# Regrouping the register loads of a column copy on VectorE and ScalarE in a graph layer

## The chip, the cores and the metric

The kernel runs on one core of one Trainium2 chip. The metric is the device time of one execution in microseconds (us). Five engines work side by side, each through its own list of instructions in order: TensorE (PE, with its weight loads PEld), VectorE (DVE), ScalarE (ACT), GpSimd (POOL) and SyncE (SP), which only issues DMAs. Besides instructions for its engine, such a list holds some that the engine's sequencer runs itself, register loads for instance; the profile gives them with a q behind the engine's name (DVEq) and does not count them as busy.

## The reference

One layer of a graph network over 12500 nodes with 64 numbers each and 212500 directed edges with 32 numbers each. The edges are sorted by destination (`dst`). All is float32.

```python
msg_in = jnp.concatenate([nodes[row], nodes[col], edge_features], axis=-1)   # row = src, col = dst
messages = relu(msg_in @ mW1 + mb1) @ mW2 + mb2
aggregated = jax.ops.segment_sum(messages, col, num_segments=nodes.shape[0])
upd = relu(jnp.concatenate([nodes, aggregated], -1) @ uW1 + ub1) @ uW2 + ub2
out = layernorm(x + upd)
```

## The kernel before

The edges are cut into 554 groups (`G`) of 384, three tiles of 128 (`TG`). A loop over `k` makes one step a group. A chain runs through each group, and one step holds work on three groups: `turn(k)`, `hidden(k - 2)` and `sums(k - 4)`.

- Gather (line 167, GpSimd). One indirect DMA a tile fetches the source nodes' 64 numbers of 128 edges into a ring of 20 groups (`own_s`, `RING`). `gather(k + 16)` is issued in step `k` and waits until TensorE has transposed the group that last held the ring's place, 20 groups earlier.
- `turn` (line 378, TensorE) transposes a group's three tiles, source nodes and one-hot places together, so that the edges stand in columns; ScalarE brings the result from PSUM to SBUF (line 389, `own_st`). A group's first tile can be left out of the gathers ("columned", below); then only its places are moved, and ScalarE needs two instructions.
- `hidden` (line 404, TensorE) multiplies by `mW1`, the window of 32 destination nodes' projections (`own_wm`) and the edges' numbers; VectorE applies the ReLU (line 415).
- `sums` (line 431, TensorE) sums the group's edges into its window of 32 nodes; VectorE adds the window to `own_agg` at an address from a register (line 458). Every fourth step also counts the edges a node has (line 442), and VectorE adds four windows of counts (line 463), each waiting for the one before.
- VectorE also makes the one-hot places of a later group (line 366).

All that TensorE does in a step waits at its first matmul: for the gathers of group `k`, for the DMAs, and for what VectorE and ScalarE did with its results two steps earlier.

The source nodes of a columned group's first 128 edges aren't gathered. All nodes lie in SBUF as columns (`own_xc`), and VectorE and ScalarE copy one column after another to its place in `own_st`, 64 partitions of 4 bytes (lines 565 and 567). The address of a column stands in a register, and the registers are filled from a list in SBUF (`index`) by `registers` (line 546): one load instruction for as many registers as it names. `fetch` then makes the copies. `VCOLS` and `ACOLS` say how many columns VectorE and ScalarE copy in a step, load by load; `COLS` is their sum. Columns are copied from step `BEGIN` = 18 until ten steps before the end, and `COPIED` (line 86) lists the groups for which a place in time is found: one group for each 128 columns. Every eighth step a new piece of the list comes by DMA (line 525, SP's queue), and VectorE turns it into addresses (line 531).

VectorE's list in a step before: ReLU (415), load of 12 (546), addition (458), in every fourth step four count additions (463), 12 copies (565), places (366), load of 8, 8 copies. The load of 12 stands between the ReLU and the addition, through the list `between`: a function put there ahead of the step is called within `add` (line 456). ScalarE's list: eviction (389), load of 12, 12 copies, load of 12, 12 copies.

As the groups close, 25 parts of the output are computed between the steps (lines 474 to 516). In the first 25 steps ScalarE also evicts a projection of all nodes (line 343), from which the windows are read. The last ten steps have no columns to copy and go through the three parts one after another.

Of the kernel before, what the change touches and what calls it, by code (L numbers as in the profile page):

```python
# [48 lines left out]
TIMES = 4  # L49
BEGIN = 18  # L50
CHECKED = 8
VCOLS = (12, 8)
ACOLS = (12, 12)
COLS = sum(VCOLS + ACOLS)
SPAN = 8


def tiles_of(g):

    n = min(GE, E - g * GE)  # L60
    return [min(P, n - j * P) for j in range((n + P - 1) // P)]
# [53 lines left out]
def ordered(ctx: ExitStack, tc: tile.TileContext, a, own, ok):  # L115
# [26 lines left out]
    def after(first, *others):  # L142

        tc.declare_no_dep(first.ins, group="quiet", reason="waits for the last of a step")
        for i in others:
            tc.add_manual_dep(
                first.ins, i.ins.name,
                mybir.DependencyInfo(mybir.DependencyClass.Sync, mybir.DependencyReason.DATA),
                reason="the kernel's own rings",
            )  # L150
        return first
# [69 lines left out]
    def bit(k):  # L221

        nodes = [NEAR_NODES + (N - NEAR_NODES) * i // BITS for i in (k, k + 1)]
        tiles = [first + (NT - first) * i // BITS for i in (k, k + 1)]
        nc.sync.dma_start(src_sb[:, slice(*tiles)], a["src"][:, slice(*tiles)])
        nc.sync.dma_start(xc[:D, slice(*nodes)], a["xT"][:, slice(*nodes)])
# [51 lines left out]
    def combined():  # L278

        wps = ups.tile([H, CH], F32, name="u_ps").rearrange("p (n h) -> p n h", n=4)  # L280
        nc.tensor.matmul(wps[:, 0], w2t, u1s, start=True, stop=True)
        nc.tensor.matmul(wps[0:1, 1], b2, u1s, start=True, stop=True)
        nc.vector.tensor_copy(wc, wps[:, 0])
        nc.vector.tensor_copy(ux[COUNT : COUNT + 1, :], wps[0:1, 1])
# [27 lines left out]
    def inputs(b):  # L312
        if b * SB >= G:
            return
        c0, c1 = b * SB * GE, min(E, (b + 1) * SB * GE)
        efs_by[b] = nc.sync.dma_start(own.st[b % BLOCKS][D + W :, : c1 - c0], a["efT"][:, c0:c1])
        after(efs_by[b], *([hidden_by[(b - BLOCKS + 1) * SB - 1]] if b >= BLOCKS else []))
# [17 lines left out]
    def projected(c):  # L335

        base, n = TABLE[c]
        ps = ups.tile([H, CH], F32, name="u_ps").rearrange("p (n h) -> p n h", n=4)
        for j in range(n):
            nc.tensor.matmul(ps[:, j], xc[: D + 1, base + j * P :][:, :P], w1b,  # L340
                             start=True, stop=True)
        t = rowp.tile([P, 4, H], F32, name="t")
        nc.scalar.activation(t[:, :n], ps[:, :n], AF.Copy)  # L343
        written.append(after(nc.sync.dma_start(
            by_dst[base : base + n * P, :].rearrange("(n p) h -> p n h", n=n), t[:, :n])))
# [79 lines left out]
    def sums(g, ps):  # L425
        h, s = own.h[g % NH], own.s[g % RING]
        sizes = tiles_of(g)
        sg = ps[2][:, : TIMES * W].rearrange("p (t w) -> p t w", w=W)
        did = []
        for j, p in enumerate(sizes):  # L430
            did.append(nc.tensor.matmul(  # L431
                sg, h[:p, j, :],
                s[:p, j, D:].unsqueeze(1).to_broadcast([p, TIMES, W]),
                start=j == 0, stop=j == len(sizes) - 1))
        counts = []
        if g % SB == SB - 1 or g == G - 1:
            g0 = g // SB * SB
            whole = [q for q in range(g0, g + 1) if tiles_of(q) == [P] * TG]
            at_ps = ps[2][0:1, TIMES * W :][:, : SB * W].rearrange("o (q w) -> o q w", w=W)
            first_s = g0 % RING  # L440
            for j in range(TG):
                did.append(nc.tensor.matmul(  # L442
                    at_ps[:, : len(whole)], own.one,
                    own.ring[:, first_s : first_s + len(whole), j, D:],
                    start=j == 0, stop=j == TG - 1))
            if len(whole) < g + 1 - g0:
                for j, p in enumerate(sizes):
                    did.append(nc.tensor.matmul(
                        at_ps[:, len(whole)], own.one[:p], s[:p, j, D:],
                        start=j == 0, stop=j == len(sizes) - 1))  # L450
            counts = [(q, at_ps[:, q - g0]) for q in range(g0, g + 1)]

        def add(step):
            sums_by[g] = step
            at = bass.ds(starts[g], W)
            if between:
                between.pop()()
            did = [after(nc.vector.tensor_tensor(agg[:, at], sg[:, 0, :], agg[:, at], ALU.add),  # L458
                         step)]
            for q, counted in counts:  # L460
                counted_by[q] = step
                count = xc[COUNT : COUNT + 1, bass.ds(starts.pop(q), W)]
                did.append(after(nc.vector.tensor_tensor(count, counted, count, ALU.add), step))  # L463
            return did

        return did, [*relu_by[g], *copy_by[g]], add
# [53 lines left out]
    def indexes(i):  # L520

        n = min(SPAN * COLS, P * len(COPIED) - i * SPAN * COLS)
        if n > 0:
            indices[i] = ixp.tile([1, SPAN * COLS], I32, name="index")
            nc.sync.dma_start(indices[i][:, :n], a["src_copied"][:, i * SPAN * COLS :][:, :n])

    def addresses(i):

        if i in indices:
            t = indices[i][:, : min(SPAN * COLS, P * len(COPIED) - i * SPAN * COLS)]  # L530
            nc.vector.tensor_scalar(t, t, 4.0, float(own.at), ALU.mult, ALU.add)

    def registers(k, *parts):

        i, n = divmod(k - BEGIN, SPAN)
        if i < 0:
            return
        all_parts = [*((ET.DVE, c) for c in VCOLS), *((ET.Activation, c) for c in ACOLS)]
        for part in parts:
            engine, count = all_parts[part]  # L540
            c0 = (k - BEGIN) * COLS + sum(c for _, c in all_parts[:part])
            count = min(count, P * len(COPIED) - c0)
            if count <= 0:
                return
            b = c0 - i * SPAN * COLS
            _, v = nc.values_load_multi_w_load_instructions(  # L546
                indices[i][0:1, b : b + count], engines=[engine],
                min_val=own.at, max_val=own.at + 4 * (N - 1),
                skip_runtime_bounds_check_because="a source is one of the nodes",
            )  # L550
            held[part] = engine, c0, v
# [60 lines left out]
        window(g)  # L612
    indexes(0)
    made = summed = 0
    between, held = [], {}

    for k in range(G):
        if k < BITS:
            bit(k)
        if 1 < k < len(TABLE):  # L620
            projected(k)
        if k == CHECKED:
            addresses(0)
            combined()
            ordered_edges()
            early.close()
            up = ctx.enter_context(tc.tile_pool(name="upd", bufs=2))
        if k % SB == 2:
            inputs(k // SB + 2)
        if k % SB == 1:  # L630
            places(k // SB + 1)
        if k < G - SHORT:
            between.append(lambda: registers(k, 0))
            step((turn, k), *([(hidden, k - 2)] if k > 1 else []),
                 *([(sums, k - 4)] if k > 3 else []))
            made, summed = max(0, k - 1), max(0, k - 3)
            if between:
                between.pop()()
            fetch(0)
        else:  # L640

            step((turn, k))
            for _ in range(2):
                if summed < made:
                    step((sums, summed))
                    summed += 1
            for _ in range(2):
                if made <= k:
                    step((hidden, made))
                    made += 1  # L650
        window(k + SB)
        onehot(k + LEAD)
        if k < G - SHORT:
            for part in range(1, len(VCOLS + ACOLS)):
                registers(k, part)
                fetch(part)
            if k >= BEGIN and (k - BEGIN) % SPAN == 0:
                indexes((k - BEGIN) // SPAN + 1)
            if k >= BEGIN and (k - BEGIN) % SPAN == SPAN - 2:
                addresses((k - BEGIN) // SPAN + 1)  # L660
        if k + AHEAD < G:
            gather(k + AHEAD)
# [330 lines left out]
```

## Time and profile before

| | |
|---|---|
| median of 3 runs | 1879.1 us (1875.58 to 1879.48) |
| profiled execution | 1872.44 us, span 1870.6 us |
| VectorE busy | 1452.9 us (78%), 13141 instructions |
| ScalarE busy | 1558.7 us (83%), 13374 instructions |
| TensorE busy | 1302.0 us (70%), weight loads 1139.3 us (61%) |
| GpSimd busy | 1400.1 us (75%), of it 1481 gathers 1399.4 us |
| column copies | 10480 on VectorE, 12560 on ScalarE |

The span is the time from the first to the last instruction; the profiled execution's own time contains it. Busy times overlap. In a row of a group stand the line, engine, operation and tiles, the count, the busy time, the mean length of one in ns, and after the second bar the engine's idle time just before these instructions with what ended it; "issue" means that the profile shows nothing that was waited for. Instructions of one engine overlap by their ends: VectorE's copies last 190 ns each, but their busy time is 884.5 us for 10480.

### The profile page before, as it was taken

To read this page: it belongs to the slowest core of one execution; us is meant where nothing else is said; L and a number is where in the kernel's file an instruction comes from. 1 tells how busy PE (TensorE), PEld (TensorE's weight loads), DVE (VectorE), ACT (ScalarE), POOL (GpSimd) and SP (SyncE) were. 2 spreads that over 40 slices of the span, in tenths; PEclk is the share of its full clock that TensorE was granted. 3 is DMA by queue.
4 is the path that set the end of the run, shared out by engine and by line. 5 is a ranking of instruction groups with operands and counts; after the bars stand their busy time and mean duration, and the time that the engine had idled before them with its cause. 6 is when DMAs were issued, how large, how long until landed. Compare 5 with 4: busy or idle time off the path is not lost. (4 is left out here: it accounts for less than half of the span.)

```text
span 1870.6 us, 55967 instructions
## 1 busy us (share of the span) xinstructions
PE 1302.0 (70%) x9839; PEld 1139.3 (61%) x9839; DVE 1452.9 (78%) x13141; ACT 1558.7 (83%) x13374; POOL 1400.1 (75%) x1488
## 2 busy tenths in 40 slices
PE   1777777677767667677676776776767767667676
PEld 0676666666666556566665666665656656556665
DVE  1338888899897888877887878888878888888773
ACT  5249999999998888888888888888888888888871
POOL 7777777777777777777777777777777777777774
PEclk9889999999999998998999998999998999999999
DMA  4543222222222222222222222222222222222221
GB/s 93 138 123 75 54 54 54 51 54 53 52 54 48 50 52 49 50 49 45 54 52 47 52 46 54 48 51 48 53 46 53 45 54 51 48 53 48 50 49 26
DMA packets 112796, 104.10 MB, mean 56 GB/s; under 512 B 51586, under 2 KB 82960, under 8 KB 112432
## 3 DMA queue, kind: packets, MB, share of 16 engines
q0 software_dynamic: 47392, 48.60, 14.8%
q1 hardware_dynamic: 64196, 51.35, 10.0%
q14 instruction: 280, 2.29, 0.4%
q8 instruction: 84, 1.38, 0.3%
q10 hardware_dynamic: 844, 0.48, 0.1%
HBM read 90.61 MB, written 9.62 MB: 54 GB/s over the span
## 5 line engine op out<-in xcount | busy, mean ns | idle before, releaser
L167 POOL DMA_INDIRECT own_s<-in_x,src_sb x1481 | 1399.4, 945 | 452.5 <-issue 342.9
L567 ACT ACTIVATE own_st<-own_xc 64x4 uint8 x12560 | 1265.6, 192 | 60.2 <-issue 52.2
L565 DVE COPY own_st<-own_xc 64x4 uint8 x10480 | 884.5, 190 | 17.3 <-issue 9.2
L378 PE MATMUL own_ps<-own_ident,own_s 128*96 128x128 f32 x1661 | 294.1, 288 | 488.7 <-DMA own_s<-in_x,src_sb 164.0
L378 PEld LDWEIGHTS own_ps<-own_ident,own_s 128*96 128x96 f32 x1661 | 169.1, 131 | 593.5 <-issue 291.0
L431 PE MATMUL own_ps<-own_s,own_h 128*128 128x128 f32 x3322 | 490.3, 287 | 1.2 <-DVE own_h L415 0.6
L404 PE MATMUL own_ps<-own_wm,own_st 128*128 128x128 f32 x3322 | 485.5, 285 | 0.0
L415 DVE TENSOR_SCALAR own_h<-own_ps 128x384 f32<-128x384 f32 x553 | 302.1, 547 | 185.5 <-PE own_ps L442 84.7
L431 PEld LDWEIGHTS own_ps<-own_s,own_h 128*128 128x128 f32 x3322 | 443.3, 203 | 2.3 <-DVE own_h L415 1.2
L404 PEld LDWEIGHTS own_ps<-own_wm,own_st 128*128 128x128 f32 x3322 | 437.8, 201 | 1.8 <-issue 1.2
L389 ACT ACTIVATE own_st<-own_ps 96x384 f32<-96x384 f32 (+2 forms) x734 | 294.2, 401 | 167.5 <-PE own_ps L442 81.6
L458 DVE TENSOR_TENSOR own_agg<-own_ps,own_agg 128x32 f32 x554 | 105.8, 191 | 170.6 <-DVE own_h L415 90.4
L366 DVE TENSOR_TENSOR own_s<-iota,dlc 128x96 f32<-128x96 f32 x554 | 136.2, 247 | 0.3 <-issue 0.2
L442 PE MATMUL own_ps<-own_s,own_one 128*1 128x128 f32 x834 | 120.6, 283 | 0.0
L463 DVE TENSOR_TENSOR own_xc<-own_ps,own_xc 1x32 f32 x554 | 101.9, 184 | 18.5 <-DVE own_xc L463 1.8
L442 PEld LDWEIGHTS own_ps<-own_s,own_one 128*1 128x1 f32 x834 | 60.2, 85 | 35.7 <-issue 3.6
L340 PE MATMUL u_ps<-w1b,own_xc 65*128 65x128 f32 x196 | 33.4, 323 | 58.1 <-ACT t L343 38.8
L340 PEld LDWEIGHTS u_ps<-w1b,own_xc 65*128 65x128 f32 x196 | 29.1, 227 | 62.3 <-ACT t L343 42.1
L343 ACT ACTIVATE t<-u_ps 128x512 f32<-128x512 f32 (+1 forms) x25 | 14.7, 588 | 58.2 <-DMA by_dst<-t 37.9
L487 PE MATMUL u_ps<-same,own_xc 65*128 65x64 f32 (+1 forms) x196 | 37.0, 271 | 1.5 <-ACT u L480 1.4
L489 PE MATMUL u_ps<-u,u 128*128 128x64 f32 (+1 forms) x196 | 38.0, 276 | 0.0
L487 PEld LDWEIGHTS u_ps<-same,own_xc 65*128 65x128 f32 (+1 forms) x196 | 29.7, 191 | 2.3 <-ACT u L480 2.2
(62 smaller groups left out, 257.1 us busy)
## 6 DMA issues: line engine op xcount, KB each, us to landing
own_st<-in_efT SPq DMA_DIRECT2D x138, 192.0 KB
own_s<-in_x,src_sb POOLq DMA_INDIRECT x1481
own_wm<-by_dst SPq DMA_DIRECT2D x554, 16.0 KB
by_dst<-t SPq DMA_DIRECT2D x24, 256.0 KB
out<-o SPq DMA_DIRECT2D x24, 128.0 KB
own_xc<-in_xT SPq DMA_DIRECT2D x12, 179.2 KB
index<-in_src_copied SPq DMA_DIRECT2D x65, 1.4 KB
dlc_i<-in_dst_cols SPq DMA_DIRECT2D x1, 831.0 KB
```

Of the source, the lines that this page charges most:

```text
L167: nc.gpsimd.indirect_dma_start(out=s[:p, j, :D], out_offset=None, in_=x[:, :], in_offset=bass.IndirectOffsetOnAxis(ap=src_sb[:p, g * TG + ...
L366: places_by[g] = nc.vector.tensor_tensor(own.s[g % RING][:, :, D:], iota.unsqueeze(1).to_broadcast([P, TG, W]), dlc[:, g * TG : (g + 1) * ...
L378: nc.tensor.transpose(xt[:, j * P : j * P + p], s[:p, j, :], ident[:p, :p])
L389: after(nc.scalar.activation(t[r, c : c + n][:, m], xt[r, m], AF.Copy), step))
L404: nc.tensor.matmul(pre[:p, j, :], t[:, c + j * P : c + j * P + p], wm[g % NW], start=True, stop=True)
L415: relu_by[g] = [nc.vector.tensor_scalar(h, pre, 0.0, None, ALU.max)]
L431: did.append(nc.tensor.matmul(sg, h[:p, j, :], s[:p, j, D:].unsqueeze(1).to_broadcast([p, TIMES, W]), start=j == 0, stop=j == len(sizes) - 1))
L442: did.append(nc.tensor.matmul(at_ps[:, : len(whole)], own.one, own.ring[:, first_s : first_s + len(whole), j, D:], start=j == 0, stop=j == ...
L458: did = [after(nc.vector.tensor_tensor(agg[:, at], sg[:, 0, :], agg[:, at], ALU.add), step)]
L463: did.append(after(nc.vector.tensor_tensor(count, counted, count, ALU.add), step))
L565: by[engine] = nc.vector.tensor_copy(o, x_at)
L567: by[engine] = nc.scalar.activation(o, x_at, AF.Copy)
```

## The change

VectorE copies 24 columns a step where it copied 20, in three loads of eight registers for one of twelve and one of eight. ScalarE copies 28 where it copied 24, in loads of 12, 8 and 8 for two of 12. `COLS` goes from 44 to 52, so the list of copied groups grows from 180 to 213, and as many tiles are not gathered. VectorE's first load is no longer called from within `add`: it comes behind the step's additions, directly ahead of its copies.

```diff
-VCOLS = (12, 8)
-ACOLS = (12, 12)
+VCOLS = (8, 8, 8)
+ACOLS = (12, 8, 8)
 COLS = sum(VCOLS + ACOLS)
...
         def add(step):
             sums_by[g] = step
             at = bass.ds(starts[g], W)
-            if between:
-                between.pop()()
             did = [after(nc.vector.tensor_tensor(agg[:, at], sg[:, 0, :], agg[:, at], ALU.add),
                          step)]
...
-    between, held = [], {}
+    held = {}
...
         if k < G - SHORT:
-            between.append(lambda: registers(k, 0))
             step((turn, k), *([(hidden, k - 2)] if k > 1 else []),
                  *([(sums, k - 4)] if k > 3 else []))
             made, summed = max(0, k - 1), max(0, k - 3)
-            if between:
-                between.pop()()
+            registers(k, 0)
             fetch(0)
```

VectorE's list in a step after: ReLU, addition, in every fourth step four count additions, load of 8, 8 copies, places, load of 8, 8 copies, load of 8, 8 copies.

## The prediction

> **What bounds the kernel now.** I read the page first, then GpSimd's timeline, then the steps by stage, and last VectorE's own row of instructions.
>
> ```profile
> span 1870.6 us, 55967 instructions
> PE 1302.0 (70%) x9839; PEld 1139.3 (61%) x9839; DVE 1452.9 (78%) x13141; ACT 1558.7 (83%) x13374; POOL 1400.1 (75%) x1488
> L167 POOL DMA_INDIRECT own_s<-in_x,src_sb x1481 | 1399.4, 945 | 452.5 <-issue 342.9
> ```
> ```profile
> 1000.83 0.94 POOL L167 DMA_INDIRECT own_s<-in_x,src_sb  x1 [0.30 <-DMA own_s<-in_x,src_sb]
> 1002.08 0.94 POOL L167 DMA_INDIRECT own_s<-in_x,src_sb  x1 [0.30 <-PE own_ps L431]
> 1003.32 0.94 POOL L167 DMA_INDIRECT own_s<-in_x,src_sb  x1 [0.30 <-issue]
> ```
>
> GpSimd looks 75% busy, but its gathers start 1.25 us apart with the same 0.30 us between them, whatever releaser is named. 1481 x 1.25 = 1851 us of a span of 1870.6: the gathers fill the whole run. With 44 columns a step copied, a step needs 3 - 44/128 = 2.656 gathers, or 3.32 us.
>
> The steps do not all run at that pace. The busy time of line 415 by stage (us of the stage, VectorE's busy time, count in brackets) counts them, since there is one ReLU a step:
>
> ```profile
> 0.00:155.00 155.00, 13.31 (x24) 0.91 0.48 116
> 155.00:520.00 365.00, 66.77 (x123) 0.99 0.25 54
> 520.00:1819.00 1299.00, 214.98 (x394) 0.95 0.24 50
> 1819.00:1871.00 52.00, 7.08 (x13) 0.92 0.14 27
> ```
>
> From 520 us on, a step takes 1299/394 = 3.30 us, the gathers' pace. Between 155 and 520 us it takes 365/123 = 2.967 us: the engines are behind the gathers there, and catch up as fast as they can. This stage shows what the engines alone allow. Its groups, and all engines' busy time in it (PE, PEld, DVE, ACT, POOL):
>
> ```profile
> 155.00:520.00 365.00, 273.02 (x2156) 238.83 (x2155) 325.90 (x3040) 353.03 (x3163) 275.98 (x293) 0.99 0.25 54
> L565 DVE COPY own_st<-own_xc 64x4 uint8 x2459 | 208.0, 189 | 4.1 <-issue 2.5
> L415 DVE TENSOR_SCALAR own_h<-own_ps 128x384 f32<-128x384 f32 x123 | 66.8, 543 | 0.8 <-PE own_ps L442 0.2 <-issue 0.2
> L389 ACT ACTIVATE own_st<-own_ps 96x384 f32<-96x384 f32 (+2 forms) x167 | 66.1, 396 | 6.3 <-PE own_ps L431 2.9 <-PE own_ps L442 2.1
> ```
>
> VectorE's ReLU waits for TensorE, and lost 0.8 us to it in 123 steps; ScalarE's eviction lost 6.3 us. So TensorE is always ahead of VectorE: VectorE sets 2.967 us, although it is busy for only 326 of the 365 us and ScalarE for 353. VectorE's missing time is in its register loads, which its sequencer runs (they aren't counted as busy). The loads of line 546, near 707 us (VectorE's two, ScalarE's two of twelve, ScalarE's last, which had eight registers; ns least/median/most, first and last start):
>
> ```profile
> L546 DVEq TENSOR_LOAD <-index x2: 592/719/846, 706.7 to 707.8; - x2
> L546 ACTq TENSOR_LOAD <-index x2: 780/781/782, 705.2 to 706.4; - x2
> L546 ACTq TENSOR_LOAD <-index x1: 549/549/549, 1814.8 to 1814.8; - x1
> ```
>
> A VectorE load of twelve takes 0.846 us, of eight 0.592: 0.064 a register and some 0.08 for the load itself. VectorE in the catching-up stage (start, length):
>
> ```profile
> 324.48 0.55 DVE L415 TENSOR_SCALAR own_h<-own_ps 128x384 f32<-128x384 f32 x1
> 325.23 0.19 DVE L458 TENSOR_TENSOR own_agg<-own_ps,own_agg 128x32 f32 x1 [0.20 <-DVE own_h L415]
> 325.33 0.93 DVE L565 COPY own_st<-own_xc 64x4 uint8 x12
> 326.18 0.24 DVE L366 TENSOR_TENSOR own_s<-iota,dlc 128x96 f32<-128x96 f32 x1
> 326.35 0.78 DVE L565 COPY own_st<-own_xc 64x4 uint8 x8
> 326.91 0.54 DVE L415 TENSOR_SCALAR own_h<-own_ps 128x384 f32<-128x384 f32 x1
> 327.65 0.19 DVE L458 TENSOR_TENSOR own_agg<-own_ps,own_agg 128x32 f32 x1 [0.20 <-issue]
> 327.85 0.84 DVE L463 TENSOR_TENSOR own_xc<-own_ps,own_xc 1x32 f32 x4
> 328.73 0.94 DVE L565 COPY own_st<-own_xc 64x4 uint8 x12
> 329.58 0.24 DVE L366 TENSOR_TENSOR own_s<-iota,dlc 128x96 f32<-128x96 f32 x1
> 329.75 0.71 DVE L565 COPY own_st<-own_xc 64x4 uint8 x8
> 330.38 0.54 DVE L415 TENSOR_SCALAR own_h<-own_ps 128x384 f32<-128x384 f32 x1
> ```
>
> A plain step is 2.43 us (324.48 to 326.91), one with the four count additions 3.47 (to 330.38). Of 2.43 us the two loads take 0.846 + 0.592 = 1.44 of the sequencer, and handing over 20 copies and four other instructions fits into the remaining 1.0. The engine's own work is less: 0.55 + 0.10 + 20 x 0.071 (twelve copies from 325.33 to 326.18) + 0.17 = 2.24. The sequencer is what is full.
>
> **The change, part by part.**
>
> *Gathers.* 52 columns a step for 44: the list of copied groups grows from 180 to 213 (line 86 worked out for both), so 33 of 1481 gathers go: 33 x 1.25 = 41 us off GpSimd's row, and a step then needs 2.594 gathers, 3.24 us. This is the whole gain; it counts only if every engine keeps that pace.
>
> *VectorE's loads.* Three of eight for one of twelve and one of eight: 3 x 0.592 - 1.438 = +0.338 us a step.
>
> *VectorE's copies.* Four more. Handing one over costs the sequencer between 0.035 us (ScalarE: loads start at 705.2 and 706.4, less the first one's 0.78 leaves 0.42 for twelve) and 0.071 (the engine's pace, if it is the limit). I take 0.035, since the engine has 0.2 us to spare in a step: +0.14, at most +0.28.
>
> *The first load behind the additions.* In a plain step its place is free: it is a load that the sequencer runs either way, and the engine then has the ReLU and the addition to work on. In every fourth step the four count additions stand in front of it, each behind the one before (0.84/4 = 0.21 us apart). Before, the load of 0.85 ran while the ReLU did; now the sequencer stands at the counts, with no load under it. From the ReLU's start to the fourth count: 0.55 + 0.2 + 3 x 0.21 = 1.4; with about 0.3 of copies still ahead of the ReLU, less the 0.2 after which a plain step's load would begin, 1.5 us a counting step. Before, a counting step costs 3.47 - 2.43 = 1.04 more, of which the counts alone are 0.84: so +0.46 to +0.66 every four steps, +0.12 to +0.16 a step. I take 0.15. The bound below is nothing: the waits do not hold the sequencer. The bound above is that each step empties the engine (a rival below).
>
> *ScalarE.* Four more copies, and loads of 12, 8 and 8 for two of 12: 0.78 + 2 x 0.549 - 1.56 = +0.32 on its sequencer.
>
> ```profile
> 708.46 0.46 ACT L389 ACTIVATE own_st<-own_ps 96x384 f32<-96x384 f32 x1
> 708.83 2.38 ACT L567 ACTIVATE own_st<-own_xc 64x4 uint8 x24
> 711.22 0.66 ACT L389 ACTIVATE own_st<-own_ps 32x128 f32<-32x128 f32 x2
> 711.78 2.38 ACT L567 ACTIVATE own_st<-own_xc 64x4 uint8 x24
> 714.06 0.47 ACT L389 ACTIVATE own_st<-own_ps 96x384 f32<-96x384 f32 x1
> ```
>
> Its steps take 2.76 and 2.84 us with copies 0.095 apart and no gap between the two groups, so its loads hide under its copies: sequencer 1.88 + 28 x 0.035 = 2.9 stays below the engine's 2.8 + 4 x 0.095 = 3.2. With what the stage adds beside the copies (2.967 less 6.3/123, so at most 2.92 before) ScalarE comes to between 3.2 and 3.3. It is late next, not first. The split evictions of 33 more groups (711.22: 0.56 for 0.37) are in that.
>
> *The rest.* The longer scaling of the indices and the refills of the index ring, on SP's queue, once in eight steps, I put at nothing: 64 more elements in one small instruction. Other queues issue what they did.
>
> *Sum.* VectorE's step: 2.967 + 0.338 + 0.14 + 0.15 = 3.59 us, above the gathers' 3.24. The gathers then run into the end of their ring and wait; the 41 us is lost. Up to 155 us, 24 steps are as before but for six that copy (+0.4 each, 3 us). 517 steps at 3.59 give 1856. The end (13 steps, 52 us, in which the gathers' pace holds now) has its gathers done: I put 45. Span: 155 + 3 + 1856 + 45 = 2059. The profiled execution takes 1872.44 for a span of 1870.6, so 2061; its time lies 0.4% below the median 1879.1 of the runs, which I leave. I say 2060.
>
> **A rule against this sum.** How a wait and the load behind it stand to each other, on ScalarE, and VectorE's copies around its load at 706.7:
>
> ```profile
> 705.23 0.49 ACT L389 ACTIVATE own_st<-own_ps 96x384 f32<-96x384 f32 x1 [2.09 <-PE own_ps L431]
> 706.10 2.45 ACT L567 ACTIVATE own_st<-own_xc 64x4 uint8 x24 [0.39 <-issue]
> ```
> ```profile
> 706.39 0.93 DVE L565 COPY own_st<-own_xc 64x4 uint8 x12
> 707.24 0.24 DVE L366 TENSOR_TENSOR own_s<-iota,dlc 128x96 f32<-128x96 f32 x1
> ```
>
> The eviction waits 2.09 us for TensorE and starts at 705.23; the load behind it starts at 705.2, not while the eviction waits, and the copies stand until it is done. The Trainium skill's page Perfetto Trace Analysis, section Per-engine timelines, says that an instruction of these two engines waits for its semaphores in a queue of its own while the sequencer already decodes the next. By that rule the 0.15 falls away. I follow the row.
>
> **The rivals.**
>
> *The waits do not hold the sequencer* (the rule above). The counts then wait beside the load: 3.44 us a step, 155 + 3 + 1778 + 45 = 1981, so 1983. Against it: the load at 705.2 that began only with the eviction.
>
> *The gathers still bound: faster.* If the three loads run beside queued copies, VectorE keeps 2.24 + 0.28 of engine work and some 0.55 for counts and the rest, about 3.1 us a step; the 41 us come through: 1831. It decides at one number: 155 + 3 + 45 + 517 s reaches 1870.6 at s = 3.225, and the gathers take over only below 3.15. That is 0.26 above the 2.967 of now, and the loads alone add 0.338 to a sequencer that the ReLU's row shows never waiting. So it needs the loads off that path.
>
> *ScalarE bounds.* With 353 us of 365 it is the busiest engine of the catching-up stage; at 3.28 us a step, 155 + 3 + 1696 + 45 = 1899, so 1901. Against it: it waits 6.3 us for TensorE where VectorE waits 0.8. The Trainium skill's Perfetto Trace Analysis, section Identifying the Most-Contended Engine, goes by occupancy, and so would name ScalarE; here the waits say VectorE, since sequencer time isn't counted as busy.
>
> *Each load empties VectorE.* Then a plain step is 0.56 to the addition, 0.67 to the first copy (a load and its 0.08), three groups of 0.57, 0.17 for line 366, and 0.2 and 0.4 of idle under the other two loads: 3.7, and with the 2.967 - 2.43 = 0.54 that a step holds beside a plain one 4.24: 155 + 3 + 2192 + 45 = 2395, so 2397. Against it: loads now start with copies still queued (at 706.7, with copies that run until 707.24).
>
> **How the numbers follow.** My forecast has 0.62, the free waits 0.18, ScalarE 0.06, the gathers 0.06, the emptied engine 0.08. With copies at 0.071, the sum's upper end is 2.967 + 0.338 + 0.28 + 0.16 = 3.75 and the span 2142; the lower end is the free waits' 1983, with a little below it: 1965 to 2145. Within 0.2% (about what these runs can tell from no change) there is only the chance that VectorE lands at 3.225: 0.01. Faster 0.06, slower 0.93.
>
> **What the profile after would show.** Right: GpSimd with gaps well over 0.30 us from a ring that is full, TensorE's step released late; line 415's ReLU never waiting, in all stages; three loads of 0.59 on VectorE; in counting steps the first copies about 0.6 us or more behind the last count; ScalarE waiting at its eviction, some 0.3 us a step. Wrong: gathers 1.25 us apart to the end, or a ReLU that waits for TensorE while ScalarE never does.

## The result and the profile after

The changed kernel takes 2093.69 us (median of 4 runs, 2088.65 to 2102.16), the kernel before beside it 1877.74. The ratio is 1.1155, with a 95% interval of 1.1116 to 1.1194: it is 11.6% slower. The prediction was 2060 us, in a range of 1965 to 2145. The profiled execution's span is 2086.9 us.

From the page of the changed kernel, its span, its busy times and the gathers:

```profile
span 2086.9 us, 61224 instructions
PE 1375.0 (66%) x9839; PEld 1203.7 (58%) x9839; DVE 1671.4 (80%) x15253; ACT 1771.4 (85%) x15519; POOL 1373.1 (66%) x1455
L167 POOL DMA_INDIRECT own_s<-in_x,src_sb x1448 | 1372.3, 948 | 632.7 <-issue 373.5
```

33 gathers are gone, and those that are left no longer fill the run. GpSimd's idle time before them rose from 452.5 to 632.7 us, and its timeline shows where: mostly 0.30 us between gathers as before, and at some of them a longer wait for TensorE, which frees the places of the ring.

```profile
1000.85 0.94 POOL L167 DMA_INDIRECT own_s<-in_x,src_sb  x1 [1.67 <-PE own_ps L431]
1002.09 0.95 POOL L167 DMA_INDIRECT own_s<-in_x,src_sb  x1 [0.30 <-issue]
...
1017.81 0.94 POOL L167 DMA_INDIRECT own_s<-in_x,src_sb  x1 [1.01 <-PE own_ps L442]
```

The ReLU's rows by stage count the steps (length of the stage, busy time, count in brackets):

```profile
0.00:155.00 155.00, 12.76 (x23) 0.92 0.49 117
155.00:520.00 365.00, 54.91 (x101) 0.92 0.22 47
520.00:2030.00 1510.00, 224.93 (x414) 0.91 0.21 45
2030.00:2087.00 57.00, 8.22 (x15) 0.90 0.05 13
```

365/101 = 3.61 us a step between 155 and 520 us, and 1510/414 = 3.647 from there to the end of the copying. There is no catching up any more: one pace rules from the start. The groups of this whole stretch, 155 to 2030 us:

```profile
L563 DVE COPY own_st<-own_xc 64x4 uint8 x12344 | 1101.5, 186 | 262.4 <-issue 210.6
L389 ACT ACTIVATE own_st<-own_ps 96x384 f32<-96x384 f32 (+2 forms) x725 | 280.9, 387 | 86.9 <-PE own_ps L431 54.6 <-PE own_ps L442 26.3
L415 DVE TENSOR_SCALAR own_h<-own_ps 128x384 f32<-128x384 f32 x515 | 279.8, 543 | 1.2 <-issue 0.6
```

VectorE's ReLU waited for nobody in 515 steps (1.2 us in all); ScalarE's evictions waited 86.9 us. VectorE's idle time stands in front of its copies, 262.4 us, most of it without a releaser: there the sequencer loads registers. VectorE's timeline, a plain step and a counting step:

```profile
1002.96 0.54 DVE L415 TENSOR_SCALAR own_h<-own_ps 128x384 f32<-128x384 f32 x1
1003.43 0.17 DVE L456 TENSOR_TENSOR own_agg<-own_ps,own_agg 128x32 f32 x1
1003.52 0.78 DVE L563 COPY own_st<-own_xc 64x4 uint8 x8
1004.09 0.24 DVE L366 TENSOR_TENSOR own_s<-iota,dlc 128x96 f32<-128x96 f32 x1
1004.46 0.69 DVE L563 COPY own_st<-own_xc 64x4 uint8 x8
1005.37 0.68 DVE L563 COPY own_st<-own_xc 64x4 uint8 x8 [0.22 <-issue]
1005.97 0.54 DVE L415 TENSOR_SCALAR own_h<-own_ps 128x384 f32<-128x384 f32 x1
1006.43 0.17 DVE L456 TENSOR_TENSOR own_agg<-own_ps,own_agg 128x32 f32 x1
1006.64 0.84 DVE L461 TENSOR_TENSOR own_xc<-own_ps,own_xc 1x32 f32 x4
1008.36 0.93 DVE L563 COPY own_st<-own_xc 64x4 uint8 x8 [0.88 <-issue]
1008.96 0.33 DVE L366 TENSOR_TENSOR own_s<-iota,dlc 128x96 f32<-128x96 f32 x1
1009.32 0.70 DVE L563 COPY own_st<-own_xc 64x4 uint8 x8
1010.23 0.66 DVE L563 COPY own_st<-own_xc 64x4 uint8 x8 [0.21 <-issue]
1010.80 0.55 DVE L415 TENSOR_SCALAR own_h<-own_ps 128x384 f32<-128x384 f32 x1
```

The plain step takes 3.01 us, the counting step 4.83, with 0.88 us of idle between the last count and the first copy. The load that stands there (ns, start), and VectorE's sequencer work and additions for the counts:

```profile
L544 DVEq TENSOR_LOAD <-index x1: 597/597/597, 1007.3 to 1007.3; - x1
L461 DVEq FUSED_REGOPS  x4: 93/96/99, 1005.8 to 1007.1; - x4
L461 DVE TENSOR_TENSOR own_xc<-own_ps,own_xc x4: 183/184/186, 1006.6 to 1007.3; 1x32 f32 x4
```

The load starts at 1007.3, with the fourth count, which had been standing at its wait for the third. It does not start when the sequencer reached the counts. The same holds in 127 of the 129 counting steps between 155 and 2030 us, where the load starts 13 to 15 ns after the fourth count does. The sequencer's own work for the fourth count's address, which reads nothing of the list, is held in the same way: it starts some 14 ns after the third count does.

The step above is unusual in one thing. Its load ends at 1007.9, and its first copy starts only at 1008.36; what filled that time isn't known. In 126 of the 129 counting steps the copy follows 0.09 us behind the load, and the idle time is 0.52 us, as here:

```profile
1502.57 0.84 DVE L461 TENSOR_TENSOR own_xc<-own_ps,own_xc 1x32 f32 x4
1503.92 0.94 DVE L563 COPY own_st<-own_xc 64x4 uint8 x8 [0.52 <-issue]
```

### The profile page after: what moved, and what is told of

It reads as the page before. It is cut to its first block, busy times and chain, and to the rows that moved or that the text cites. A ratio compares the mean times of both kernels' runs of the same rounds, so it can differ in the third digit from the quotient of the medians.

```text
span 2086.9 us, 61224 instructions
## 1 busy us (share of the span) xinstructions
PE 1375.0 (66%) x9839; PEld 1203.7 (58%) x9839; DVE 1671.4 (80%) x15253; ACT 1771.4 (85%) x15519; POOL 1373.1 (66%) x1455
## 5 line engine op out<-in xcount | busy, mean ns | idle before, releaser
L167 POOL DMA_INDIRECT own_s<-in_x,src_sb x1448 | 1372.3, 948 | 632.7 <-issue 373.5
L565 ACT ACTIVATE own_st<-own_xc 64x4 uint8 x14672 | 1461.9, 191 | 85.3 <-issue 60.2
L563 DVE COPY own_st<-own_xc 64x4 uint8 x12592 | 1123.2, 186 | 271.9 <-issue 219.3
L378 PE MATMUL own_ps<-own_ident,own_s 128*96 128x128 f32 x1661 | 307.9, 299 | 602.9 <-ACT own_st L389 381.7
L431 PE MATMUL own_ps<-own_s,own_h 128*128 128x128 f32 x3322 | 522.4, 300 | 5.7 <-DVE own_h L415 3.0
L404 PE MATMUL own_ps<-own_wm,own_st 128*128 128x128 f32 x3322 | 515.4, 297 | 0.0
L431 PEld LDWEIGHTS own_ps<-own_s,own_h 128*128 128x128 f32 x3322 | 473.8, 215 | 8.3 <-DVE own_h L415 4.6
L404 PEld LDWEIGHTS own_ps<-own_wm,own_st 128*128 128x128 f32 x3322 | 468.1, 213 | 2.2 <-issue 1.2
L456 DVE TENSOR_TENSOR own_agg<-own_ps,own_agg 128x32 f32 x554 | 97.0, 175 | 11.0 <-PE own_ps L431 5.6
L472 PE MATMUL u_ps<-own_agg,wc 128*128 128x512 f32 (+1 forms) x50 | 27.9, 640 | 27.6 <-DVE own_agg L456 27.6
```

Of the source, the lines that this page charges most:

```text
L167: nc.gpsimd.indirect_dma_start(out=s[:p, j, :D], out_offset=None, in_=x[:, :], in_offset=bass.IndirectOffsetOnAxis(ap=src_sb[:p, g * TG + ...
L378: nc.tensor.transpose(xt[:, j * P : j * P + p], s[:p, j, :], ident[:p, :p])
L404: nc.tensor.matmul(pre[:p, j, :], t[:, c + j * P : c + j * P + p], wm[g % NW], start=True, stop=True)
L431: did.append(nc.tensor.matmul(sg, h[:p, j, :], s[:p, j, D:].unsqueeze(1).to_broadcast([p, TIMES, W]), start=j == 0, stop=j == len(sizes) - 1))
L563: by[engine] = nc.vector.tensor_copy(o, x_at)
L565: by[engine] = nc.scalar.activation(o, x_at, AF.Copy)
```

## The experiments

The theory under test: VectorE's sequencer sets the step, by its loads and copies and by the place of the first load. The main rivals: ScalarE's larger share does it; the place costs nothing; the waits do not hold the sequencer. The first seven runs stood beside a kernel before of 1873 us.

**The old place with the new columns** (undo_place).

```diff
 # the kernel before, with
-VCOLS = (12, 8)
-ACOLS = (12, 12)
+VCOLS = (8, 8, 8)
+ACOLS = (12, 8, 8)
```

> The changed kernel, but VectorE's first load called from within the additions again, ahead of them (the old place, the new columns). Theory (VectorE's sequencer sets the step, and the counts stand in front of the load): the placement is worth 0.15 to 0.25 us of the changed kernel's 3.65 us a step, so 3.40 to 3.50 us in the stage from 520 us on and a time near 155 + 3 + 517 x 3.45 + 57 = 2000 us (1975 to 2030); a counting step is about 1.0 longer than a plain one, not 1.8. Rival (the place is worth nothing, only loads and copies cost): 3.65 us a step and 2090 us. Rival (ScalarE sets the step): the same 2090 us.

Measured: 2010.43 us against 1873.62, ratio 1.0741 (1.0723 to 1.0759). The ReLU's rows from 520 us on, and for the whole stretch in which columns are copied:

```profile
520.00:1800.00 1280.00, 200.91 (x370) 0.93 0.22 47
155.00:1940.00 1785.00, 279.71 (x515) 0.94 0.22 47
```

From 520 us on, 1280/370 = 3.459 us a step: the place is worth 3.647 - 3.459 = 0.188 us, and all else 3.459 - 2.967 = 0.492. Over the same 515 steps of both kernels it is 1785/515 = 3.466 against 1875/515 = 3.641: 0.175 for the place and 0.499 for all else. The 2.967 could be read only between 155 and 520 us. A counting step in this kernel's timeline:

```profile
1008.92 0.54 DVE L415 TENSOR_SCALAR own_h<-own_ps 128x384 f32<-128x384 f32 x1
1009.39 0.19 DVE L458 TENSOR_TENSOR own_agg<-own_ps,own_agg 128x32 f32 x1
1009.59 0.84 DVE L463 TENSOR_TENSOR own_xc<-own_ps,own_xc 1x32 f32 x4
1010.46 0.66 DVE L565 COPY own_st<-own_xc 64x4 uint8 x8
```

The copies follow the last count without a gap: the load has been done ahead of the additions. Sorted by kind over this stretch, 288 plain steps take 3.13 us on average here and 3.16 in the changed kernel, 128 counting steps 3.91 and 4.55, and 98 steps with other work on VectorE 3.90 and 3.89. The place costs the counting steps 0.64 us each, which is 0.16 us a step, and the plain ones next to nothing.

**VectorE's part without ScalarE's** (vector_only).

```diff
 # the changed kernel, with
-ACOLS = (12, 8, 8)
+ACOLS = (12, 12)
```

> The changed kernel with ScalarE's old share: VectorE 24 columns in three loads of eight behind the additions, ScalarE 24 in two loads of 12; 48 columns a step. Theory: VectorE's list is the changed kernel's, so its step is too: 3.6 to 3.7 us and 2070 to 2100 us, with ScalarE waiting about 0.5 us a step at its evictions. Rival (ScalarE sets the step, and its four columns and third load are what costs): ScalarE is back at 2.9 us or less, the gathers (3 - 48/128 = 2.625 a step, 3.28 us) bound again, and the time is near 1860 us.

Measured: 2087.28 us, ratio 1.1133 (1.1088 to 1.1177); 3.647 us a step from 520 us on (1280/351), the changed kernel's figure. The ReLU's row, and then its ReLUs and evictions from the view of their lines between 155 and 1800 us (with what their engine sat idle for, us and times):

```profile
520.00:1800.00 1280.00, 190.20 (x351) 0.92 0.21 45
L415 DVE TENSOR_SCALAR own_h<-own_ps x451: 523/541/559, 155.1 to 1795.8; 128x384 f32<-128x384 f32 x151
  issue: 0.5, 2
L389 ACT ACTIVATE own_st<-own_ps x623: 268/381/488, 155.8 to 1799.6; 96x384 f32<-96x384 f32 x72, 32x128 f32<-32x128 f32 x42, 96x256 f32<-96x256 f32 x42
  PE own_ps L431: 107.6, 137
  PE own_ps L442: 50.4, 52
```

ScalarE has four copies and a load less a step, and waits more (158 us for 451 steps, 0.35 us each); the step doesn't move. ScalarE's share has no part in the loss.

**ScalarE's part alone** (scalar_only).

```diff
 # the kernel before, with
-ACOLS = (12, 12)
+ACOLS = (12, 8, 8)
```

> The kernel before with ScalarE's new share alone: 28 columns in loads of 12, 8 and 8; VectorE as before with its load ahead of the additions; 48 columns a step. Theory: VectorE needs 2.97 us a step, ScalarE 3.2 to 3.3, the gathers 3.28. ScalarE becomes the bound of the stage from 155 to 520 us and hardly catches up: 155 + 2 + 517 x 3.25 + 52 = 1889 us (1860 to 1910), within some 1% of before. Rival (ScalarE's share is what made the change slow): 3.6 us a step and 2080 us.

Measured: 1853.99 us against 1873.62, ratio 0.99 (0.9883 to 0.9916): 1.0% faster than the kernel before. It has 16 gathers less, and 16 x 1.25 = 20 us is what it gained; the expected 1889 was too slow by the pace assumed for ScalarE (3.25). Its groups between 155 and 1800 us:

```profile
L567 ACT ACTIVATE own_st<-own_xc 64x4 uint8 x14409 | 1423.4, 195 | 3.0 <-issue 2.9
L415 DVE TENSOR_SCALAR own_h<-own_ps 128x384 f32<-128x384 f32 x515 | 281.0, 546 | 76.9 <-PE own_ps L442 74.9 <-issue 0.8 <-PE own_ps L431 0.3
L389 ACT ACTIVATE own_st<-own_ps 96x384 f32<-96x384 f32 (+2 forms) x708 | 277.1, 391 | 6.8 <-PE own_ps L442 1.9
```

Now ScalarE is the one that hardly waits (6.8 us in 708 evictions), and VectorE's ReLU loses 76.9 us. 515 steps in 1645 us are 3.19 us, just under the gathers' 2.625 x 1.25 = 3.28, so the engines catch up by the end. ScalarE's extra loads hide under its copies: 3.0 us of idle ahead of 14409 of them.

**The place alone** (place_only): the changed kernel with `VCOLS = (12, 8)` and `ACOLS = (12, 12)`.

> The kernel before with VectorE's first load (of twelve) behind the additions and nothing else; 44 columns a step. Theory: VectorE's own pace, seen in the stage from 155 to 520 us, goes from 2.967 to between 3.1 and 3.2 us a step, still below the gathers' 3.32, so the time stays within 0.5% of before (1870 to 1885 us) and the catching up takes longer. Rival (the load in front of the additions held VectorE up, and its new place frees it): the stage's step falls below 2.9 us. Rival (the place alone is what made the change slow): over 1950 us.

Measured: 1873.18 us against 1873.62, ratio 0.9995 (0.9986 to 1.0005): no difference. The stage from 155 to 520 us:

```profile
155.00:520.00 365.00, 64.09 (x118) 0.98 0.25 52
```

365/118 = 3.093 us a step for 2.967: VectorE's own pace is 0.126 us worse, and the gathers' 3.32 hide it. (By kind, plain steps take 2.61 us both here and before; counting steps 3.98 and 3.52.) A wait moved to a worse place costs nothing until the engine has no time left.

**Fewer loads for the same columns** (two_loads).

```diff
 # the changed kernel, with
-VCOLS = (8, 8, 8)
+VCOLS = (12, 12)
```

> The changed kernel with VectorE's same 24 columns in two loads of 12 in place of three of eight; the first load still behind the additions. Theory (the sequencer's time is the step): 2 x 0.848 for 3 x 0.592 is 0.08 us less a step, so 3.56 us and some 2045 us (2035 to 2065). Rival (short loads are better because the engine stands less under each): 2094 us or more, with longer idle times ahead of the copies.

Measured: 2026.38 us, ratio 1.0823 (1.0796 to 1.085); 3.516 us a step (1280 us, 364 steps). This is faster than the 2035 to 2065 us that the theory gave: one load less brings 0.131 us a step, more than the 0.08 that its own length explains. By kind, plain steps gain 0.16 and counting steps 0.02; in the latter the longer first load stands in full behind the counts (0.77 us of idle for 0.52). Why plain steps gain twice the length isn't explained. Shorter loads are not better here.

**No count additions** (no_counts).

```diff
             for q, counted in counts:
                 counted_by[q] = step
-                count = xc[COUNT : COUNT + 1, bass.ds(starts.pop(q), W)]
-                did.append(after(nc.vector.tensor_tensor(count, counted, count, ALU.add), step))
+                starts.pop(q)
```

> The changed kernel without VectorE's count additions in every fourth step (line 461 is left out, so the bias of the second layer is not added for the edges; TensorE's counting stays). Theory (the sequencer stands at each count and the load behind them starts only then): a counting step, 4.55 us where a plain one is 3.16, becomes a plain one, so 1.39 / 4 = 0.35 us a step goes: 3.30 us and about 155 + 517 x 3.30 + 55 = 1916 us (1890 to 1940). Rival (the counts wait beside the load, and only their 0.84 us on the engine counts at most): at most 0.21 us a step goes: 3.43 us or more, 1985 us or more.

The kernel leaves the four additions out, so that the bias of the second layer is missing from the sums over edges.

Measured: 1901.42 us, ratio 1.0151 (1.0134 to 1.0168).

```profile
520.00:1800.00 1280.00, 212.04 (x391) 0.97 0.23 50
```

1280/391 = 3.274 us a step is 0.37 less than in the changed kernel, where the additions' own 0.84 us every four steps are 0.21. The other 0.16 is what the counting steps lost by the load's place.

**49 columns** (balanced): the kernel before with `VCOLS = (10, 12)` and `ACOLS = (12, 8, 7)`.

> The kernel before with 49 columns a step: VectorE 22 in loads of 10 and 12, the first called ahead of the additions as before; ScalarE 27 in loads of 12, 8 and 7. 1461 gathers for 1481. Theory: VectorE's loads are 0.13 us longer and it has two more copies: 2.97 + 0.13 + 0.07 = 3.17 us, ScalarE about 3.10 (3.19 with 28 columns), the gathers 3.27: they bound, and 20 x 1.25 = 25 us go against before: 1849 us (1843 to 1858), a little under the kernel with ScalarE's share alone (1854). Rival (VectorE's added share does not fit): 1870 us or more.

Measured: 3376.24 us, ratio 1.802: the expectation failed by far. The register loads of this kernel (ns least/median/most):

```profile
L546 ACTq TENSOR_LOAD <-index x1566: 544/1735/3122, 124.0 to 3321.9; - x196
L546 DVEq TENSOR_LOAD <-index x1046: 849/2292/3235, 123.0 to 3320.2; - x175
```

The instructions of the engines are as long as ever, but the loads are up to some three times as long. Sorted by the place of a load's first number in the list, VectorE's loads of 12 take 0.85 us where that place is a multiple of four and 2.72 to 2.74 elsewhere; ScalarE's loads of eight 0.55 and 1.74 to 1.77. In all kernels before, every load started at a multiple of four and named a multiple of four registers; with 49 columns a step and loads of 10 and 7, only one load in four starts so.

**The list one number further on** (shifted), to see whether the start alone does it:

```diff
 # the kernel before, with
-            indices[i] = ixp.tile([1, SPAN * COLS], I32, name="index")
+            indices[i] = ixp.tile([1, SPAN * COLS + 8], I32, name="index")[:, 1:]
```

> The kernel before with its list of addresses one number further on in its tile, so that no load starts at a multiple of four numbers; nothing else. If the start decides a load's length, as the loads of the kernel with 49 columns suggest (VectorE's of 12: 0.85 us at multiples of four, 2.73 elsewhere; ScalarE's of 12: 0.79 and 2.60), ScalarE's sequencer needs 2 x 2.6 + 24 x 0.035 = 6.1 us a step and the time is near 155 + 517 x 6.2 + 55 = 3415 us (3200 to 3600). If the 49 columns' slowness was of another cause: 1870 to 1885 us.

Measured: 3438.01 us. Its loads:

```profile
L546 DVEq TENSOR_LOAD <-index x1048: 1837/2564/3353, 169.7 to 3384.3; - x175
L546 ACTq TENSOR_LOAD <-index x1047: 1751/2593/3165, 169.7 to 3384.3; - x175
```

The ReLU's row:

```profile
520.00:3300.00 2780.00, 246.44 (x452) 0.69 0.13 27
```

ScalarE's loads of 12 go from 0.78 to a median of 2.59 us with nothing changed but where they start, and a step takes 2780/452 = 6.15 us where 6.2 had been worked out from that. This run and the next four are from two later occasions, on which the kernel before took 2434 and 2445 us; why it did isn't known, and there is no trace of it from there. That the whole time lies so near the 3415 us expected may therefore be partly luck; the lengths of the loads do not depend on it.

**A copy's and a load's price by themselves** (fewer_copies, three_loads, each twice), to split the 0.492 us. In fewer_copies the third load of VectorE fills eight registers, of which four are copied from (`v[:4] if part == 2 else v`); three_loads is the changed kernel with `VCOLS = (8, 8, 4)` and `ACOLS = (12, 12)`.

> The changed kernel with all its loads, but of VectorE's third load only four columns are copied and four are left out (so their places in the features hold what stood there before). It takes the four added copies away and leaves the loads. If handing over is what a copy costs (0.035 us each): 3.64 less 0.14 = 3.50 us a step, some 2020 us (2010 to 2040). If it is the engine's 0.071 us each: 3.36 us and 1945 us. If the loads alone set the step: 2090 us.

> The kernel before with VectorE's same 20 columns in loads of 8, 8 and 4, the first behind the additions as in the changed kernel; ScalarE as before; 44 columns a step. It adds one load to the kernel with the place alone, whose stage from 155 to 520 us has 365/118 = 3.09 us a step. By a load's own length (0.08 beside its registers) that stage comes to 3.17; by what one load less brought at 24 columns (3.65 to 3.52 us) to 3.22. The whole stays with the gathers at 3.32: 1870 to 1885 us.

> The same kernel as in the run before it, with four of VectorE's 24 columns loaded and not copied, on another occasion: there the kernel before itself took 2445 us. If handing over is what a copy costs (0.035 us each): 3.64 less 0.14 = 3.50 us a step, some 2020 us (2010 to 2040). If it is the engine's 0.071 us each: 3.36 us and 1945 us. If the loads alone set the step: 2090 us.

> Again VectorE's 20 columns in loads of 8, 8 and 4, the first behind the additions, ScalarE as before: the stage from 155 to 520 us at 3.17 us a step by a load's own length, 3.22 by what one load less brought at 24 columns; the whole with the gathers, 1870 to 1885 us.

Measured: fewer_copies 2492.82 and 2493.31 us, ratios 1.0187 and 1.0261; three_loads 2464.3 and 2457.96, ratios 1.0087 and 1.0109, each to a kernel before of 2434 to 2445. All are out of what any theory expected; the theories went by times read on the occasion when the kernel before took 1873 us. The instructions kept their lengths, but the engines stood without a releaser far more often; ScalarE's and VectorE's copies in the first three_loads run:

```profile
L565 ACT ACTIVATE own_st<-own_xc 64x4 uint8 x12560 | 1357.0, 192 | 480.4 <-issue 469.8 <-DMA by_dst<-t 1.0
L563 DVE COPY own_st<-own_xc 64x4 uint8 x10480 | 964.0, 189 | 453.3 <-issue 393.1 <-DMA by_dst<-t 0.8
```

470 us of "issue" stand here for 52.2 in the trace of the kernel before, which is from the earlier occasion. In this run ScalarE's copies stop 614 times, by 0.50 us in the median, with no load between them; the traces of the kernel before and of the changed kernel have no such stop. What held the sequencers isn't known, and these runs don't settle the price of a copy.

Traces of the earlier occasion give an estimate of it. In the changed kernel, the end of VectorE's second load and the start of its third, with eight copies between, lie 0.31 to 0.33 us apart in 473 of 514 steps: 0.040 us a copy. From the first load's end to the second's start, with the places (line 366) as well, the median is 0.36 us with eight copies there and 0.47 with twelve in two_loads: 0.028 a copy. Four copies come to 0.11 to 0.16 us by that.

## Why the prediction was right, point by point

- *What bounds the kernel.* That VectorE sets the pace whenever the gathers don't, though ScalarE is busier, was read from the ReLU's 0.8 us of waiting against the eviction's 6.3. For the kernel before, place_only bears it out: a change in VectorE's list alone moves the step between 155 and 520 us from 2.967 to 3.093. For the changed kernel, vector_only shows it: ScalarE's share taken back, the step stays at 3.647.
- *Loads and copies, +0.338 and +0.14.* Together 0.478 us; undo_place shows 0.49 to 0.50. The sum holds. Of its parts, the copies' 0.14 lies within the estimate of 0.11 to 0.16 from the traces; the loads' part is less sure, since one load less brought 0.131 where 0.08 was reckoned.
- *The first load behind the additions, +0.15.* Right in kind and place: plain steps hardly feel it, counting steps do. The size was a little low: 0.175 with the new columns over the 515 steps (0.188 from 520 us on), 0.126 with the old ones between 155 and 520 us. The counting step lost 0.64 and 0.46 us, the two ends of the estimate of 0.46 to 0.66. The first copies were to come 0.6 us or more behind the last count; 0.52 us is the rule.
- *ScalarE late next.* Right: 3.19 us a step in scalar_only, where it is first. It was put at 3.2 to 3.3, and its waiting in the changed kernel at 0.3 us a step where it is 86.9/515 = 0.17.
- *Gathers.* Their ring fills and the 41 us is lost: GpSimd waits for TensorE.
- *The sum.* 155 + 3 + 1856 + 45 = 2059 against 155 + 1875 + 57 = 2087. The stretch with columns took 515 steps at 3.641 us for 517 at 3.59, 19 us more: the place is 0.025 over its term and the columns 0.02. The end took 57 us for 15 steps, where 45 were put down for 13. The 3 us for the six steps that copy before 155 us show as one step less there, 23 for 24.
- *The rivals.* Waits that don't hold the sequencer would have left the place without a price. undo_place shows that it has one, and the load at 1007.3, with its like in 127 of 129 counting steps, and no_counts (0.37 us a step gone, more than the 0.21 of the additions themselves) show why: the wait in front of a register load held that load. By that, the statement of the Trainium skill's Perfetto Trace Analysis, Per-engine timelines, that the sequencer goes on while an instruction waits, did not hold for these loads. The occupancy rule of the same page, Identifying the Most-Contended Engine, would have named ScalarE in the changed kernel too (85% against 80%); vector_only disagrees. The gathers bound again, and an engine emptied at each load (4.24 us a step), did not come about.

## What to carry to other kernels

Count what an engine's sequencer does by itself, register loads above all, as work of that engine: it is not in the busy time, and an engine at 80% with a full sequencer is the bound when its first instruction of each step never waits. Put such a load where an engine instruction runs anyway, not behind a chain of instructions that wait for each other (0.64 us a counting step here). When a bound is relieved by handing work to other engines, give it to the one with time left: four columns more on ScalarE gained 1.0%; with four more on VectorE too, in one load more, the kernel was 7.4% slower than before, and 11.6% with the first load behind the counts as well.

## What was not expected of the hardware

A register load of twelve numbers takes 0.85 us on VectorE and 0.79 on ScalarE when its first number stands at a multiple of four in the list, and 2.73 and 2.60 us when it does not. Loads whose number of registers is no multiple of four pay for the rest: ten registers from a multiple of four took 1.08 us on VectorE, where eight take 0.59 and twelve 0.85; seven on ScalarE 0.97, where eight take 0.55. In these runs the lengths on VectorE fit loads that go by fours from a start at a multiple of four, at 0.25 us a four, and take the left-over numbers singly, at 0.24 us each. From any other start all numbers seem to go singly: 1.84 us for eight and 2.72 for twelve in shifted, 0.22 us a number. Loads like these turned a kernel expected at 1849 us into one of 3376.
